# Expert layer: the shares of the experts spread over partitions by a transfer through DRAM instead of by TensorE products, with the router run further ahead

## The chip, the cores and the metric

The program runs on one core of one Trainium2 chip. Its engines are TensorE (PE, with its weight loads, PEld), VectorE (DVE), ScalarE (ACT), GpSimd (POOL) and SyncE (SP, which here only issues transfers). They run side by side, each takes its own instructions in order, and they wait for each other through semaphores. The metric is the device time of one execution in microseconds (us); "before" is the median of three runs.

## The reference, cut to what matters

The whole program is a network of twelve residual stages on a tensor `x` of 8 sequences x 512 tokens x 128 features. Only the stage with experts changes; it occurs twice, as the fourth and the sixth stage:

```python
    x = x + 0.5 * _L1_ffn_ref(_layernorm(x, axis=-1), ...)
...
        # 16 experts of 64 features, 4 chosen for a token, from 2 of 4 groups
        logits = xf @ gate_w.T
        scores = jax.nn.sigmoid(logits)
        sfc = scores + gate_bias
        ...
        topk_w = topk_w / (topk_w.sum(-1, keepdims=True) + 1e-20)
        topk_w = topk_w * SCALE
        cw = (jax.nn.one_hot(topk_idx, E, dtype=topk_w.dtype) * topk_w[..., None]).sum(1)
        hg = jnp.einsum('nh,eih->nei', xf, Wg)
        hu = jnp.einsum('nh,eih->nei', xf, Wu)
        act = jax.nn.silu(hg) * hu
        y = jnp.einsum('nei,ne,ehi->nh', act, cw, Wd)
        shared = jax.nn.silu(xf @ Ws_g.T) * (xf @ Ws_u.T) @ Ws_d.T
        y = y + shared
        return (x + y.reshape(b, s, h)).astype(hidden_states.dtype)
```

Here `cw` holds for each token the shares of the 16 experts: 0 for those that were not chosen, and otherwise the normalized score times 2.5. Every one of an expert's 64 features is multiplied by that token's share.

## The kernel before, in words

`x` stays in SBUF for the whole program, with tokens on the partitions (128 tokens x 4 chunks x 128 features for a sequence). The expert stage is `l1_ffn`. It works through the eight sequences in turn, and for each there are two generators, `routed` and `experts`, which `l1_ffn` steps in turn: one step of `experts(b)`, then one step of `routed(b + 1)`.

`experts(b)` computes with features on the partitions and the 512 tokens of the sequence along the free axis. All 16 experts are computed for every token. Two experts of 64 features fill the 128 partitions, so there are eight pairs, and as a ninth the shared expert. For each pair `e`, TensorE makes `pg` and `pu` (each a 128x512 product in float32, which runs as two passes, so the profile counts it as two instructions), ScalarE writes `act = silu(pg)`, VectorE multiplies `act` by `pu`, and then by the shares of the pair's two experts. TensorE multiplies the result by the down weights and sums over the nine into the PSUM bank `po`. At the end ScalarE copies `po` to `yT`, four transposes on TensorE turn it back to tokens, and VectorE adds it to `x` (`y`, then `add_half`).

The shares come out of the router with tokens on the partitions. `experts` needs the share of one expert along the tokens, and the same on all the 64 partitions of that expert's features. Before the change TensorE does that spreading: `shares` is a constant matrix of zeros and ones, and `pw = shares x shareT` (line 768, 32 rows against 128 columns, 512 tokens) repeats each row over 64 partitions. So that this keeps float32 precision[...], the share is cut in two terms, `share_lead` and `share_trail` (lines 723 to 726), which lie side by side in `halves` (copied four times by POOL, line 729, so that products can start from different row groups) and are transposed together (line 735). VectorE multiplies by `pw` in line 770.

`routed(b)` does what comes ahead of it: the layer norm of the sequence (`norm`: statistics and scaling on VectorE, the power -1/2 on POOL), four transposes and a copy on ScalarE to `xT` (tile `mm`, one PSUM bank that all transposes and router products share), and `route`: the products for the 16 scores, the sigmoid on ScalarE (a table of its own, so tables are loaded before and after it), then some 25 small VectorE instructions that rank groups and experts. The costly ones compare all pairs of 16 experts: two comparisons, a product on POOL (line 799), a maximum and a sum (lines 795 to 801). Last, the scores of the chosen are normalized to `share` (lines 847 to 853).

What order the instructions have on each engine is not that of the source: a scheduling layer takes the traced instructions, estimates their times and puts them in an order for each engine, and buffers are handed out from pools of a fixed number (`bufs`). A tile that wants a buffer in use waits for its last reader. Only in the second sequence (`b == 1`) are POOL and VectorE kept in the order of the source; there the steps of `aside`, which make constants for the attention stage that follows, are placed between. PSUM[...]: `mm` 1, `po` 1, `pg`, `pu` and `pw` 2 each. The buffers of `act` are 3.

SP issues the loads of weights. In the neighbourhood of the two stages it has one each: `w_ffn<-in_l2f` at the first's beginning, `w_mixer<-in_l3a` at the second's.

Of the kernel before, what the change touches and what calls it, by code (L numbers as in the profile page):

```python
# [25 lines left out]
P = 128  # L26
# [70 lines left out]
def _packs(i):  # L97
# [56 lines left out]
    p.add("spread", np.tile(np.repeat(np.eye(16, dtype=np.float32), 64, axis=1), (8, 1)))  # L154
# [68 lines left out]
class _Kernel:  # L223
# [459 lines left out]
    def l1_ffn(self):  # L683
# [3 lines left out]
        with ExitStack() as s:  # L687
            keep = s.enter_context(tc.tile_pool(name="keep", bufs=1))
            self.sb = s.enter_context(tc.tile_pool(name="sb", bufs=2))
            self.ps = s.enter_context(tc.tile_pool(name="ps", bufs=2, space=bass.MemoryType.PSUM))  # L690
            self.shares = keep.tile([P, 8, P], F32R, name="shares")
            nc.vector.tensor_copy(
                self.shares.rearrange("p e m -> p (e m)"), self.w["moe", "spread"]
            )
            self.seqs = [{} for _ in range(NB)]
            for _ in self.routed(0):
                pass
            for b in range(NB):
                ahead = self.routed(b + 1) if b + 1 < NB else iter(())
                experts = self.experts(b)  # L700
                for _ in range(10):
                    with self.in_order(*(() if b != 1 else (mybir.EngineType.Pool, mybir.EngineType.DVE))):
                        next(experts)
                        next(ahead, None)
                        if b == 1:
                            next(self.aside, None)
                for _ in ahead:
                    pass

    def routed(self, b):  # L710


        nc, sb, ps = self.nc, self.sb, self.ps
        q = self.seqs[b]
        q["xn"] = self.norm(self.x[b], self.ln_pool)
        yield
        xT = sb.tile([P, L], F32, name="xT")
# [5 lines left out]
        lead = sb.tile([P, NC, 16], F32R, name="share_lead")  # L723
        nc.vector.tensor_copy(lead, share)
        trail = sb.tile([P, NC, 16], F32, name="share_trail")
        nc.vector.tensor_tensor(trail, share, lead.bitcast(F32), ALU.subtract)
        halves = sb.tile([P, NC, 4, 2, 16], F32, name="halves")
        for k, t in enumerate((lead.bitcast(F32), trail)):
            nc.gpsimd.tensor_copy(
                halves[:, :, :, k, :], t.unsqueeze(2).to_broadcast([P, NC, 4, 16])  # L730
            )
        yield
        pt = ps.tile([P, NC, P], F32, name="mm", bufs=1)
        for c in range(NC):
            nc.tensor.transpose(
                pt[:, c, :], halves[:, c].rearrange("p r k e -> p (r k e)"), self.ident
            )
        q["shareT"] = sb.tile([P, L], F32R, name="shareT")
        nc.scalar.copy(q["shareT"], pt.rearrange("p c t -> p (c t)"))
        yield  # L740

    def experts(self, b):
# [11 lines left out]
        last = None  # L754
        for e in range(9):
            pg = ps.tile([P, L], F32, name="pg")
            self.mm(pg, w("w_g")[:, bass.ts(e, P)] if e < 8 else w("ws_g"), xT)
            pu = ps.tile([P, L], F32, name="pu")
            self.mm(pu, w("w_u")[:, bass.ts(e, P)] if e < 8 else w("ws_u"), xT)
            act = sb.tile([P, L], F32, name="act", bufs=3)  # L760
            nc.scalar.activation(act, pg, AF.Silu)  # L761
            nc.vector.tensor_tensor(act, act, pu, ALU.mult)  # L762
            if e < 8:
                if e % 2 == 0:
                    pw = []
                    for k in range(e, e + 2):
                        r = bass.ts(k % 4, 32)
                        pw.append(ps.tile([P, L], F32, name="pw"))
                        self.mm(pw[-1], self.shares[r, k, :], q["shareT"][r, :])
                nc.vector.tensor_tensor(act, act, pw[e % 2], ALU.mult)  # L770
            if last is not None:
                down(*last)
            last = (e, act)
            yield
        down(*last)
# [751 lines left out]
```

## Time and profile before

| | us |
|---|---|
| median of three runs | 2550.56 (2547.38 to 2552.48) |
| the profiled execution | 2548.84 |
| its span, from the first instruction to the last | 2547.1 |
| first expert stage, sequence 0 ends (copy of `yT`) | 596.56 |
| first expert stage, sequence 7 ends | 801.44 |
| second expert stage, sequence 0 ends | 1361.02 |
| second expert stage, sequence 7 ends | 1563.82 |
| busy in the whole span: PE, DVE, ACT, POOL | 2172.6, 1667.3, 1289.9, 645.0 |
| PE products `pw`, both stages | 128, of about 0.49 each |

A row of the profile such as "L770 DVE TENSOR_TENSOR act<-act,pw 128x512" is an instruction or a group: line of the kernel, engine, operation, what it writes and what it reads, and its size. In a timeline the first number is the start in us from the span's beginning and the second the length; "x2" says that two alike were put together; in brackets stands how long the engine was idle ahead of it, and what released it. In a table of windows each row gives the window's bounds and length and then, for PE, PEld, DVE, ACT and POOL, the busy time in it (with the number of instructions), the clock that TensorE was granted as a share of full speed, the share of time in which the transfer engines were busy, and GB/s. Lines of a matrix product or transpose are those of helpers (L256, L338), so products are told apart by the tiles that they write.

### The profile page before, as it was taken

Reading aid. Unit: us, or ns where it says so; the run is one execution under the profiler, and the core shown is the slowest. Engines: PE = TensorE matmul, PEld = TensorE weight load, DVE = VectorE, ACT = ScalarE, POOL = GpSimd, SP = SyncE. Lnnn points to the kernel's source line nnn. Section 1 sums busy time; section 2 is a strip of 40 time slices with the busy share of each in tenths; the row PEclk is TensorE's granted clock in tenths of the full one; section 3 lists DMA queues with packets and bytes.
Section 4 is the critical chain, followed back from the end, with each engine's and each line's share of the span. In section 5 each row is a group of like instructions: output and inputs, shape, how many; then the busy total and the mean of one; then the engine's idle time right before and its main releaser. Section 6 shows DMA issues by size and latency. Waiting matters only on the chain.

```text
span 2547.1 us, 30527 instructions
## 1 busy us (share of the span) xinstructions
PE 2172.6 (85%) x10959; PEld 1050.6 (41%) x10959; DVE 1667.3 (65%) x3908; ACT 1289.9 (51%) x2055; POOL 645.0 (25%) x916
## 2 busy tenths in 40 slices
PE   7579899879998988998879997763477999999989
PEld 3434444334444433333334443541354444444444
DVE  4565555468776888888638777975885466566611
ACT  3278787323332276777743333447343425555554
POOL 1122333112112011111122113545453112333330
PEclk9689798989999699999989998976788969999989
DMA  3000000000000000000000000000000000000001
GB/s 115 1 1 1 1 1 1 13 9 1 1 1 1 0 1 1 1 1 1 1 7 1 1 1 1 1 1 0 1 1 1 0 1 1 2 1 1 1 1 33
DMA packets 10039, 13.10 MB, mean 5 GB/s; under 512 B 416, under 2 KB 8736, under 8 KB 9760
## 3 DMA queue, kind: packets, MB, share of 16 engines
q1 hardware_dynamic: 7776, 10.11, 1.2%
q8 instruction: 86, 1.41, 0.2%
q10 hardware_dynamic: 2112, 1.05, 0.2%
q14 instruction: 65, 0.53, 0.1%
HBM read 9.06 MB, written 2.10 MB: 4 GB/s over the span
## 4 chain that ended last, share of the span: by engine, by line
PE 60%; DVE 18%; ACT 10%; POOL 7%; issue 4%; DMA 0%; ACTq 0%; DVEq 0%; POOLq 0%; SPq 0%
PE pair L256 11%; PE av L256 8%; PE po L256 8%; PE first L256 7%; PE pg L256 5%; PE pu L256 4%; PE ck L256 4%; PE mm L256 4%; DVE max L1282 3%; ACT e L1390 3%; PE ph L256 2%; POOL xn_rstd L271 1%; DVE xn L282 1%; PE pw L256 1%; PE pi L256 1%
## 5 line engine op out<-in xcount | busy, mean ns | idle before, releaser
L1282 DVE TENSOR_REDUCE max<-first 128x1 f32<-128x512 f32 (+3 forms) x864 | 534.9, 664 | 186.9 <-PE first L256 182.7
L1390 ACT ACTIVATE e<-pair 128x1024 f32<-128x1024 f32 (+3 forms) x512 | 436.4, 864 | 243.1 <-PE pair L256 230.8
L256 PE MATMUL first<-qkT 32*128 32x512 f32 (+3 forms) x1024 | 335.7, 471 | 32.8 <-DVE max L1282 32.1
L256 PE MATMUL pair<-qkT 32*128 32x512 f32 (+3 forms) x1024 | 223.3, 454 | 19.0 <-ACT e L1390 13.9
L256 PE MATMUL av<-e,v 128*32 128x512 f32 (+3 forms) x2048 | 237.8, 534 | 0.1
L761 ACT ACTIVATE act<-pg 128x512 f32<-128x512 f32 x144 | 86.0, 597 | 234.7 <-PE pg L256 186.0
L256 PE MATMUL pair<-mT,max_rows 32*128 32x512 f32 (+3 forms) x1024 | 191.0, 374 | 1.8 <-DVE mT L1324 1.8
L256 PEld LDWEIGHTS first<-qkT 32*128 32x128 f32 x1024 | 151.5, 196 | 97.8 <-DVE max L1282 89.7
L256 PEld LDWEIGHTS pair<-qkT 32*128 32x128 f32 x1024 | 95.4, 185 | 232.2 <-ACT e L1390 131.8
L1392 POOL TENSOR_SCALAR_AFFINE_SELECT e<-e 128x256 f32<-128x256 f32 x256 | 103.4, 407 | 251.7 <-ACT e L1390 251.4
L256 PE MATMUL po<-act,w_moe 128*128 128x512 f32 x288 | 157.3, 632 | 3.0 <-DVE act L770 1.9
L256 PE MATMUL pg<-xT,w_moe 128*128 128x512 f32 x288 | 153.5, 616 | 0.0
L256 PE MATMUL pu<-xT,w_moe 128*128 128x512 f32 x288 | 149.3, 601 | 0.0
L762 DVE TENSOR_TENSOR act<-act,pu 128x512 f32<-128x512 f32 x144 | 98.2, 682 | 49.0 <-PE pu L256 47.1
L1288 POOL COPY copies<-max 128x128 f32<-128x128 f32 x64 | 22.6, 410 | 341.0 <-DVE max L1282 341.0
L339 ACT COPY xT<-mm 128x512 f32<-128x512 f32 x80 | 46.4, 584 | 114.7 <-PE mm L338 102.4
L271 POOL TENSOR_TENSOR xn_rstd<-xn_rs,nhalf 128x4 f32<-128x4 f32 x80 | 88.9, 1111 | 54.4 <-ACT xn L277 35.2
L256 PEld LDWEIGHTS pair<-mT,max_rows 32*128 32x128 f32 x1024 | 96.8, 188 | 3.6 <-DVE mT L1324 3.3
L770 DVE TENSOR_TENSOR act<-act,pw 128x512 f32<-128x512 f32 x128 | 87.1, 682 | 16.5 <-PE pw L256 15.0
L282 DVE TENSOR_SCALAR xn<-x,xn_mv,xn_rstd 128x128 f32<-128x128 f32 x224 | 69.4, 370 | 39.4 <-POOL xn_rstd L271 27.9
L338 PE MATMUL mm<-w_const,xn 128*128 128x128 f32 x256 | 53.6, 331 | 48.0 <-DVE xn L282 43.6
L269 POOL TENSOR_SCALAR xn_rs<-xn_mv 128x4 f32<-128x4 f32 x80 | 20.4, 256 | 291.3 <-DVE xn_mv L267 289.7
(339 smaller groups left out, 4349.3 us busy)
## 6 DMA issues: line engine op xcount, KB each, us to landing
w_moe<-in_moe SPq DMA_DIRECT2D x1, 2392.0 KB, 14.0
out<-x SPq DMA_DIRECT2D x8, 256.0 KB, 2.3
x<-in_u ACTq DMA_DIRECT2D x4, 256.0 KB, 6.7
x<-in_u SPq DMA_DIRECT2D x4, 256.0 KB, 6.5
w_mixer<-in_l0a SPq DMA_DIRECT2D x1, 954.5 KB, 8.2
w_mixer<-in_l1a SPq DMA_DIRECT2D x1, 769.0 KB, 4.1
w_ffn<-in_l0f SPq DMA_DIRECT2D x1, 578.0 KB, 7.3
w_ffn<-in_l2f SPq DMA_DIRECT2D x1, 560.0 KB, 3.5
```

Source lines behind the costliest of these rows:

```text
L256: self.nc.tensor.matmul(out, lhsT, rhs, start=start, stop=stop)
L271: nc.gpsimd.tensor_tensor(rstd, rs, self.nhalf[:, :n], ALU.pow)
L282: nc.vector.tensor_scalar(xn[:, c, :], x[:, c, :], mv[:, c, 0:1], rstd[:, c : c + 1], ALU.subtract, ALU.mult)
L338: self.nc.tensor.transpose(pt[:, c, :], xn[:, c, :], self.ident)
L339: copy(out, pt.rearrange("p c t -> p (c t)"))
L761: nc.scalar.activation(act, pg, AF.Silu)
L762: nc.vector.tensor_tensor(act, act, pu, ALU.mult)
L770: nc.vector.tensor_tensor(act, act, pw[e % 2], ALU.mult)
L1282: nc.vector.tensor_reduce(mx[:, c, j, gs[0] : gs[-1] + 1], sc, AX.X, ALU.max, negate=True)
L1288: nc.gpsimd.tensor_copy(copies[:, :, :, :, g], mx[:, :, :, g].unsqueeze(3).to_broadcast([P, NC, 4, 8]),)
L1390: nc.scalar.activation(e[:, :, :n], sc[:, :, :n], AF.Exp, scale=scale)
L1392: nc.gpsimd.affine_select(e[:, :, :P], e[:, :, :P], pattern=[[0, 2], [1, P]], compare_op=ALU.is_ge, fill=0.0, base=0, channel_multiplier=-1,)
```

## The change: what it does

The share is no longer cut in two and spread by TensorE. It is transposed once per chunk to 16 rows (one for each expert), copied by ScalarE to `shareT` (16 partitions x 512 tokens), and written by SP to a DRAM tile of 32 KB, `shares`. SP then issues two transfers back from it into `share_wide`, a tile of 128 partitions x 8 pairs x 512 tokens (2 MB, 16 KB in a partition, two buffers): the first gives the rows of the even experts to each of partitions 0 to 63, the second those of the odd experts to partitions 64 to 127. VectorE multiplies `act` by a slice of `share_wide`. The constant `spread` (1024 columns of the weights) and its cast into `shares` are gone.

The routers form one chain of steps, of which 15 run ahead of the first `experts`: all of router 0 and, of router 1, everything up to the ranks. A router has nine steps and `experts` takes ten, so the lead grows by a step with each sequence. Because `pw` leaves two PSUM banks, `pg` and `pu` have three each; `act` has five buffers, and the down product follows its expert by three instead of one. The normalized sequence has its own tile `routed_xn` with three buffers, and `xT` has three too.

```diff
@@ -151,7 +151,6 @@
-    p.add("spread", np.tile(np.repeat(np.eye(16, dtype=np.float32), 64, axis=1), (8, 1)))
@@ -685,58 +684,57 @@
-            self.shares = keep.tile([P, 8, P], F32R, name="shares")
-            nc.vector.tensor_copy(
-                self.shares.rearrange("p e m -> p (e m)"), self.w["moe", "spread"]
+            self.dram = s.enter_context(
+                tc.tile_pool(name="dram", bufs=2, space=bass.MemoryType.DRAM)
             )
             self.seqs = [{} for _ in range(NB)]
-            for _ in self.routed(0):
-                pass
+            ahead = (step for b in range(NB) for step in self.routed(b))
+            for _ in range(15):
+                next(ahead)
             for b in range(NB):
-                ahead = self.routed(b + 1) if b + 1 < NB else iter(())
                 experts = self.experts(b)
                 for _ in range(10):
...
-                for _ in ahead:
-                    pass
...
-        q["xn"] = self.norm(self.x[b], self.ln_pool)
+        q["xn"] = self.norm(
+            self.x[b], self.ln_pool, out=sb.tile([P, NC, D], F32, name="routed_xn", bufs=3)
+        )
         yield
-        xT = sb.tile([P, L], F32, name="xT")
+        xT = sb.tile([P, L], F32, name="xT", bufs=3)
...
         share = out[0]
-        lead = sb.tile([P, NC, 16], F32R, name="share_lead")
-        nc.vector.tensor_copy(lead, share)
-        trail = sb.tile([P, NC, 16], F32, name="share_trail")
-        nc.vector.tensor_tensor(trail, share, lead.bitcast(F32), ALU.subtract)
-        halves = sb.tile([P, NC, 4, 2, 16], F32, name="halves")
-        for k, t in enumerate((lead.bitcast(F32), trail)):
-            nc.gpsimd.tensor_copy(
-                halves[:, :, :, k, :], t.unsqueeze(2).to_broadcast([P, NC, 4, 16])
-            )
-        yield
         pt = ps.tile([P, NC, P], F32, name="mm", bufs=1)
         for c in range(NC):
-            nc.tensor.transpose(
-                pt[:, c, :], halves[:, c].rearrange("p r k e -> p (r k e)"), self.ident
+            nc.tensor.transpose(pt[:16, c, :], share[:, c, :], self.ident)
+        shareT = sb.tile([16, L], F32, name="shareT")
+        nc.scalar.copy(shareT, pt[:16].rearrange("p c t -> p (c t)"))
+        rows = self.dram.tile([16, L], F32, name="shares")
+        nc.sync.dma_start(out=rows, in_=shareT)
+        q["share"] = sb.tile([P, 8, L], F32, name="share_wide")
+        pairs = rows.rearrange("(e k) t -> k e t", k=2)
+        for k in range(2):
+            nc.sync.dma_start(
+                out=q["share"][bass.ts(k, 64)],
+                in_=pairs[k].unsqueeze(0).to_broadcast([64, 8, L]),
             )
-        q["shareT"] = sb.tile([P, L], F32R, name="shareT")
-        nc.scalar.copy(q["shareT"], pt.rearrange("p c t -> p (c t)"))
+        yield
+        yield
         yield
@@ -751,28 +749,23 @@
-        last = None
+        acts = []
         for e in range(9):
-            pg = ps.tile([P, L], F32, name="pg")
+            pg = ps.tile([P, L], F32, name="pg", bufs=3)
...
-            act = sb.tile([P, L], F32, name="act", bufs=3)
+            act = sb.tile([P, L], F32, name="act", bufs=5)
             nc.scalar.activation(act, pg, AF.Silu)
             nc.vector.tensor_tensor(act, act, pu, ALU.mult)
             if e < 8:
-                if e % 2 == 0:
-                    pw = []
-                    for k in range(e, e + 2):
-                        r = bass.ts(k % 4, 32)
-                        pw.append(ps.tile([P, L], F32, name="pw"))
-                        self.mm(pw[-1], self.shares[r, k, :], q["shareT"][r, :])
-                nc.vector.tensor_tensor(act, act, pw[e % 2], ALU.mult)
-            if last is not None:
-                down(*last)
-            last = (e, act)
+                nc.vector.tensor_tensor(act, act, q["share"][:, e, :], ALU.mult)
+            acts.append((e, act))
+            if len(acts) > 3:
+                down(*acts.pop(0))
             yield
-        down(*last)
+        for last in acts:
+            down(*last)
```

## The prediction

> **What bounds the kernel now.** I read the summary of the page first, then a table of windows cut at the end of each sequence of the two expert stages (a sequence ends when ScalarE copies `yT`), then the timeline inside one sequence, then the timeline of the stage's start, and last the DMA issues. The first expert stage runs from about 545 to 803 us, the second from about 1309 to 1566 us; nothing else in the kernel is touched. The table, first stage, sequences 1 to 7 (columns: length, busy time of PE, weight loads, DVE, ACT, POOL, then granted clock):
>
> ```profile
> 596.56:629.53 32.97, 31.19 (x87) 13.46 (x86) 27.45 (x79) 10.52 (x17) 9.71 (x12) 1.00 0.00 0
> ...
> 715.29:744.91 29.62, 29.62 (x83) 12.78 (x82) 22.48 (x59) 9.81 (x15) 4.67 (x7) 1.00 0.00 1
> 744.91:774.54 29.63, 29.63 (x83) 12.78 (x82) 22.48 (x59) 9.81 (x16) 4.68 (x7) 1.00 0.00 1
> 774.54:801.44 26.90, 26.81 (x70) 11.01 (x68) 14.71 (x31) 6.44 (x11) 2.28 (x5) 1.00 0.00 1
> sum 204.88, PE 202.14 PEld 86.63 DVE 157.18 ACT 64.87 POOL 41.37; mean PE 28.88 PEld 12.38 DVE 22.45 ACT 9.27 POOL 5.91
> ```
>
> PE is busy for all of 29.62 us, at full clock; the second stage's seven windows sum to 202.8 us with PE busy 201.05. So TensorE work taken out comes off the time, until VectorE (22.48 of 29.62) fills up. What a share product costs, from the timeline of PE (start, length):
>
> ```profile
> 728.88 1.02 PE L256 MATMUL pu<-xT,w_moe 128*128 128x512 f32 x2
> 729.83 0.50 PE L256 MATMUL pw<-shareT,shares 32*128 32x512 f32 x1
> 730.26 1.12 PE L256 MATMUL pg<-xT,w_moe 128*128 128x512 f32 x2
> 731.32 0.50 PE L256 MATMUL pw<-shareT,shares 32*128 32x512 f32 x1
> 731.75 1.12 PE L256 MATMUL po<-act,w_moe 128*128 128x512 f32 x2
> 732.71 1.02 PE L256 MATMUL pu<-xT,w_moe 128*128 128x512 f32 x2
> ```
>
> A 128x512 product starts 0.857 us after the one before it where nothing lies between. From 728.88 to 732.71 are three of them and two `pw`: 3.83 - 3 x 0.857 = 1.26, or 0.63 us per `pw` slot. Two `pw` side by side (different row groups) fill one slot; the window from 715.29 has six slots.
>
> [...] No transfer here has 64 partitions; the trace's 128-partition loads reach 769 KB in 4.1 us. [...] one `xn` of normally 0.34 us took 1.80 beside a fill on POOL.
>
> ```profile
> 547.11 1.80 POOL L1092 MEMSET v<- 128x2048 f32 x1
> 547.19 1.80 DVE L282 TENSOR_SCALAR xn<-x,xn_mv,xn_rstd 128x128 f32<-128x128 f32 x1 [0.93 <-POOL xn_rstd L271]
> ```
>
> **Removed.** PE: all `pw`. Counting the instructions of the changed order between the `yT` transposes of sequences 0 and 7, first stage: 188 products of 0.857 = 161.1 us, and the small ones at their spacing in the window from 715.29 (6 share transposes of 0.43, 5 `xn` transposes of 0.44, 5 router products of 0.81, 7 `yT` of 0.58 = 12.9): 174.0 us, against 204.88 now. Second stage 174.1 against 202.8. So 30.9 and 28.7 us of cover are bought. DVE loses `share_lead` and `share_trail` (0.46 us a sequence) and the cast of `shares` (2.08 us, of which about 0.8 lay on the first stage's start). POOL loses `halves` (0.8 us, and 1.1 us of the router's chain). `act*pw` becomes `act*share` with both inputs in SBUF: 0.69 us for such a product (`fc`), 0.68 now; nothing.
>
> **Added: the DMA path, per sequence.** ScalarE copies 16 rows (0.58), SP stores 32 KB, waits for it, issues two reads of 1 MiB. Store: 2.3 us, the row of `out<-x`.
>
> ```profile
> out<-x SPq DMA_DIRECT2D x8, 256.0 KB, 2.3
> ...
> w_mixer<-in_l1a SPq DMA_DIRECT2D x1, 769.0 KB, 4.1
> ```
>
> Reads, from below: 1024 packets of 2 KB at the 85 ns that a 2068-byte packet of `w_heads` takes, over 16 engines: 5.4 us[...] Where the order puts the first `po` that needs it, 24 products (20.6 us) and 1.7 us of small ones lie between for sequences 2 to 4, more after: 22 us. Hidden, by 6 us. If it were not, `act*share` stands ahead of the next `act*pu` on DVE, `pu`'s three banks fill, and PE stops. SP carries nothing else there: the load of `l2f` was issued at 543.25, that of `l3a` at 1317.32, both ahead of the first share.
>
> **Added: the stage's start.** Now:
>
> ```profile
> 568.78 0.20 DVE L853 TENSOR_SCALAR share<-share 128x64 f32<-128x64 f32 x1
> ...
> 571.27 0.58 ACT L739 CAST shareT<-mm 128x512 fp32r<-128x512 f32 x1 [10.48 <-PE mm L735]
> ...
> 572.73 1.28 DVE L770 TENSOR_TENSOR act<-act,pw 128x512 f32<-128x512 f32 x2 [3.27 <-PE pw L256]
> 573.47 0.50 PEld L256 LDWEIGHTS po<-act,w_moe 128*128 128x128 f32 x2 [0.56 <-DVE act L770]
> 573.47 2.07 PE L256 MATMUL po<-act,w_moe 128*128 128x512 f32 x2 [0.15 <-DVE act L770]
> ```
>
> In the changed order PE does 16 products of sequence 0 first (10 now), and DVE does two `act*pu` and four `xn` more ahead of the share: ready at 568.98 - 0.8 + 1.2 + 1.0 = 570.4, copied by 572.4. But then, on DVE, router 1 complete and three instructions of router 2 stand ahead of the first `act*share`. With durations of router 0: `xn` transposes 1.1, copy 0.6, router product 1.9 (cold), sigmoid 0.25, router chain 12.7 (554.14 to 569.0 less its three `act*pu` and the waits they bring), share transposes 1.1, copy 0.6, then for router 2 again 1.1, 0.6, 1.9, 0.25, and 0.4 = 22.5 us: 594.9. The DMAs land at about 586, so they are not what is late; DVE's order is. First `po` at 595.7 against 573.47; from there 9 `po` and one `pg`, `pu` are left. 11 products are 9.4 us, and about 3 more because the clock is cold (now too, products go at half rate from 572 to 578): `yT` of sequence 0 at 608.2 against 596.56, 11.6 late. Second stage, without the cast's 0.8: 12.4 late, 1373.4 against 1361.02.
>
> **Added: VectorE close to full.** Summing the changed DVE order by the spacings of before (products 0.60, router's wide ones 1.15, waits for POOL's 2.36 us product where too little stands between) against PE, between updates of `x`: 39.2 to 36.1, 25.2 to 24.5, 28.3 to 25.4, 24.3 to 22.8, then PE is longer. Excess 8.2 us; second stage 4.4. The share's transposes stand in PE's queue, so PE waits when DVE is late. Blocking of `act*share` by POOL is estimated at 0.4 us a sequence and left out.
>
> **Sum.** First stage: 608.2 + 174.0 + 8.2 = 790.4 against 801.44, -11.0. Second: 1373.4 + 174.1 + 4.4 = 1551.9 against 1563.8, -11.9. Together -22.9 on the profiled execution's 2548.84 us (span 2547.1): 2525.9. The median of the runs, 2550.56, lies 1.7 higher: 2528.
>
> **Rivals.** (1) Slower: the reads[...]: four late in sequences 1 to 4 of each stage, and about 1 at the start, less where DVE's excess overlaps: some 14 us a stage, 28 in all, +5: 2556. It decides from about 19.5 us for the two reads (108 GB/s); at 50 GB/s the reads outlast a sequence and cost over 100 us. For it: nothing of this kind in the trace. Against: packets of 2 KB run at their 85 ns here. (2) No difference: DVE and PE wait for each other in turns, beyond the sums: 1.3 us a sequence more, 14 sequences, 18 us: 2546. For it: DVE at 92% by my sums, and its order puts few products into POOL's 2.36 us. Against: five `act` buffers and three of `pg`, `pu`. (3) Better: the start costs 4 us a stage and DVE hides: -(30.9 + 28.7) + 8 + 4 = -47: 2503. Against it, DVE's order at the start is fixed.
>
> **Chances and range.** Main case 0.68, (1) 0.15, (2) 0.10, (3) 0.07. Two runs 0.2% apart are what this kernel's measurement can tell from no change, 5.1 us. Faster: main but for 0.01, plus (3), plus a little of (2): 0.76. Same: 0.09. Slower: 0.15. Range 2510 to 2553: main, (2) and the near edge of (1). Main alone: 2514 to 2542.
>
> **What would show it.** No `pw`; windows of 22 to 28 us; first `act*share` near 595 and 1359 with PE idle some 15 us before it, released by DVE's router, not by a DMA; two reads landing within 12 us; PE waits on the share's transposes in the first four sequences. A first `act*share` of later sequences released by a DMA means rival 1. Shorter starts mean that I misread DVE's order.

## The result, and the profile after

The changed kernel takes 2539.25 us in the median of 20 runs (2531.5 to 2553.41), against 2548.75 us for the kernel before, run beside it; the ratio is 0.9969 with a 95% interval of 0.9954 to 0.9983. That is 7.9 us less (4.3 to 11.7; the ratio is that of the means, and the medians alone lie 9.5 us apart), where 22.9 were forecast: faster, but by a third of the forecast, and inside its range.

The profiled execution of the changed kernel took 2550.71 us (span 2549.0), longer than most of its runs, but a second profile of the same instructions (run 12 below, 2538.47 us) gave the four lengths in the table again to within 0.02 us, so the difference lies outside the stages. The two stages are therefore measured here from marks in their own neighbourhood: the last update of `x` ahead of the first stage; ahead of the second, VectorE's `o`, which takes up the last projection of the attention; and the copies of `yT`. "Start" is from the mark to the first `yT`, "steady" from the first to the eighth `yT`.

| us | start, stage 1 | steady, stage 1 | start, stage 2 | steady, stage 2 | sum |
|---|---|---|---|---|---|
| before | 50.99 | 204.88 | 52.26 | 202.80 | 510.93 |
| after | 60.64 | 188.80 | 63.86 | 191.45 | 504.75 |
| forecast for the change | +11.6 | -22.7 | +12.4 | -24.3 | -23 |
| measured for the change | +9.65 | -16.1 | +11.6 | -11.4 | -6.2 |

The starts came nearly as forecast. The steady stretches lost 46.9 us in the forecast and 27.4 on the chip: there the missing gain lies. The windows of the changed kernel's first stage, cut at `yT` as before:

```profile
611.05:638.72 27.67, 26.24 (x75) 12.00 (x74) 24.28 (x78) 9.91 (x15) 8.35 (x10) 1.00 0.40 78
638.72:666.89 28.17, 26.86 (x75) 11.82 (x74) 25.60 (x77) 9.92 (x15) 8.64 (x8) 1.00 0.38 76
...
723.24:752.03 28.79, 25.49 (x73) 11.43 (x72) 25.76 (x60) 9.32 (x15) 4.50 (x5) 1.00 0.38 75
752.03:776.15 24.12, 24.12 (x63) 10.83 (x62) 14.95 (x33) 6.54 (x12) 1.26 (x2) 1.00 0.45 88
776.15:799.85 23.70, 23.61 (x58) 10.19 (x56) 13.40 (x23) 5.96 (x10) 0.00 (x0) 1.00 0.00 1
sum 188.80, PE 179.92 PEld 80.31 DVE 150.38 ACT 62.08 POOL 35.80; mean PE 25.70 PEld 11.47 DVE 21.48 ACT 8.87 POOL 5.12
```

In the last two windows no router is left: TensorE is busy throughout, and a sequence takes 23.7 to 24.1 us. With a router in it a sequence takes 27 to 29, and neither TensorE nor VectorE is busy all of that time. What they wait for, in the steady stretch of stage 1 (the columns: total, times, longest):

```profile
POOL ge L792 <- DVE ge L790: 32.3, 9, 5.7
DVE act L760 <- PE pu L255: 12.8, 14, 1.2
DVE gt L793 <- POOL ge L792: 9.9, 7, 2.5
PEld po L255 <- DVE act L762: 7.0, 8, 1.9
PE mm L723 <- DVE share L846: 4.8, 5, 1.6
```

VectorE stands for GpSimd's product (9.9 us) and for TensorE's `pu` (12.8); TensorE stands for VectorE's `act*share` and, at the share's transposes, for its router. One such place from the timeline of stage 2, in the sequence that took 32.56 us:

```profile
1449.72 1.22 DVE L790 TENSOR_TENSOR ge<-masked 128x1024 f32<-128x1024 f32 x1
...
1451.02 2.73 POOL L792 TENSOR_TENSOR ge<-ge,w_moe 128x1024 f32<-128x1024 f32 x1 [2.84 <-DVE ge L790]
1451.46 0.68 DVE L760 TENSOR_TENSOR act<-act,pu 128x512 f32<-128x512 f32 x1
...
1453.79 1.23 DVE L793 TENSOR_TENSOR gt<-gt,ge 128x1024 f32<-128x1024 f32 x1 [1.65 <-POOL ge L792]
1454.93 0.68 DVE L762 TENSOR_TENSOR act<-act,share_wide 128x512 f32<-128x512 f32 x1
...
1455.67 1.15 PE L255 MATMUL po<-act,w_moe 128*128 128x512 f32 x2 [2.09 <-DVE act L762]
...
1456.63 1.89 PE L255 MATMUL pu<-xT,w_moe 128*128 128x512 f32 x2
...
1458.32 1.89 PE L255 MATMUL po<-act,w_moe 128*128 128x512 f32 x2
```

The `act*share` that TensorE needs had its inputs at 1452.2, but stands behind the maximum, which waits for GpSimd. TensorE stops for 2.09 us, and the products after it run at half rate for 3 to 4 us (1.69 us from one to the next at 1456.63, where 0.857 is usual; the table in the last section shows the clock there). The start, as the forecast described it (first stage):

```profile
575.22 0.20 DVE L846 TENSOR_SCALAR share<-share 128x64 f32<-128x64 f32 x1
...
576.71 0.57 ACT L725 COPY shareT<-mm 16x512 f32<-16x512 f32 x1 [7.51 <-PE mm L723]
...
592.12 0.20 DVE L846 TENSOR_SCALAR share<-share 128x64 f32<-128x64 f32 x1
...
598.62 3.09 DVE L762 TENSOR_TENSOR act<-act,share_wide 128x512 f32<-128x512 f32 x5
599.36 6.50 PE L255 MATMUL po<-act,w_moe 128*128 128x512 f32 x10 [1.55 <-DVE act L762]
```

Router 1 is done at 592.3 and three instructions of router 2 follow before the first `act*share`, at 48.2 us behind the mark (49.3 forecast). No wait for a transfer stands before it: SP issued the first of the two reads at 578.96 and the second at 579.68, and even at the longest time below, 12.5 us, both have landed by about 592. The time that the reads took, over both stages, from the query for the tile `share_wide`:

```profile
DMA to landing us min/median/max: 7.6/10.2/12.5
```

### The profile page after: what moved, and what is told of

It is laid out like the page before. It is cut to its first block, busy times and chain, and to the rows that moved or that the text cites. A ratio compares the mean times of both kernels' runs of the same rounds, so it can differ in the third digit from the quotient of the medians.

```text
span 2549.0 us, 30187 instructions
## 1 busy us (share of the span) xinstructions
PE 2135.1 (84%) x10786; PEld 1045.3 (41%) x10831; DVE 1659.8 (65%) x3874; ACT 1285.9 (50%) x2051; POOL 636.1 (25%) x884
## 4 chain that ended last, share of the span: by engine, by line
PE 54%; DVE 22%; ACT 10%; POOL 9%; issue 6%; DMA 0%; ACTq 0%; DVEq 0%; POOLq 0%; SPq 0%
PE pair L255 11%; PE av L255 8%; PE first L255 7%; PE po L255 6%; PE ck L255 4%; PE mm L255 3%; DVE max L1275 3%; ACT e L1383 3%; PE pg L255 3%; PE pu L255 3%; PE ph L255 2%; POOL xn_rstd L270 2%; DVE act L760 1%; POOL ge L792 1%; DVE xn L281 1%
## 5 line engine op out<-in xcount | busy, mean ns | idle before, releaser
L255 PE MATMUL po<-act,w_moe 128*128 128x512 f32 x288 | 147.7, 621 | 11.4 <-DVE act L762 10.1
L760 DVE TENSOR_TENSOR act<-act,pu 128x512 f32<-128x512 f32 x144 | 97.6, 680 | 29.2 <-PE pu L255 27.1
L1281 POOL COPY copies<-max 128x128 f32<-128x128 f32 x64 | 22.7, 410 | 344.8 <-DVE max L1275 344.8
L265 DVE BATCH_NORM_STATS2 xn_st<-x 128x6 f32<-128x128 f32 x320 | 80.5, 271 | 16.4 <-POOL x L1456 7.3
L762 DVE TENSOR_TENSOR act<-act,share_wide 128x512 f32<-128x512 f32 x128 | 89.8, 709 | 0.9
L255 PEld LDWEIGHTS po<-act,w_moe 128*128 128x128 f32 x288 | 54.5, 198 | 82.6 <-issue 45.8
## 6 DMA issues: line engine op xcount, KB each, us to landing
share_wide<-shares SPq DMA_DIRECT2D x32, 1024.0 KB, 10.2
w_moe<-in_moe SPq DMA_DIRECT2D x1, 1880.0 KB, 12.4
```

What stands on the lines that cost most here:

```text
L255: self.nc.tensor.matmul(out, lhsT, rhs, start=start, stop=stop)
L265: nc.vector.bn_stats(st[:, c, :], x[:, c, :])
L762: nc.vector.tensor_tensor(act, act, q["share"][:, e, :], ALU.mult)
```

## The experiments

Four theories were written down. **T** (turns): VectorE waits for GpSimd's product, TensorE for VectorE, VectorE for TensorE; that is what the steady stretch costs. **F** (full): VectorE simply has too much to do. **L** (lock): `act*share`, with two SBUF inputs, is shut out while GpSimd works (up to 2.35 us for one in the changed kernel, where the median is 0.68). **S** against **D**: the start is set by the order of the instructions, or by the transfers. In all runs marked "order held" the order of every engine's instructions within both stages was forced to that of the kernel it derives from, so that one thing alone changes; a list in the source does this, and shifts its line numbers. In this table "half clock" is how long TensorE's clock was granted at half within the two steady stretches, and the ratio is that of whole runs to the kernel before.

| run | start 1 | steady 1 | start 2 | steady 2 | half clock 1, 2 | ratio (95%) |
|---|---|---|---|---|---|---|
| after | 60.64 | 188.80 | 63.86 | 191.45 | 0, 3.4 | 0.9969 (0.9954-0.9983) |
| 1 no product | 56.69 | 179.07 | 60.12 | 179.63 | 0, 0 | 0.9833 (0.9813-0.9853) |
| 2 product on VectorE | 57.49 | 186.35 | 61.39 | 186.93 | 0, 0 | 0.9898 (0.9880-0.9915) |
| 3 no lock | 60.68 | 187.89 | 63.88 | 190.04 | 0, 3.4 | 0.9943 (0.9924-0.9962) |
| 4 sequence 0 by TensorE | 63.17 | 188.90 | 64.66 | 187.77 | 0, 0 | 0.9944 (0.9924-0.9964) |
| 5 start reordered | 55.89 | 190.07 | 58.72 | 193.61 | 0, 6.8 | 0.9912 (0.9897-0.9927) |
| 6 norm early | 60.65 | 186.51 | 59.45 | 189.51 | 0, 3.4 | 0.9954 (0.9939-0.9969) |
| 7 reads twice | 64.29 | 212.95 | 68.49 | 211.50 | 23.9, 23.9 | 1.0173 (1.0156-1.0190) |
| 8 before, no `pw` | 49.22 | 203.95 | 50.76 | 201.80 | 6.8, 6.8 | 0.9981 (0.9969-0.9992) |
| 9 before, lag 3 | 52.20 | 208.85 | 53.44 | 208.12 | 0, 0 | 1.0053 (1.0036-1.0069) |
| 10 before, no `pw`, lag 3 | 36.73 | 197.08 | 36.82 | 196.50 | 6.8, 3.4 | 0.9826 (0.9807-0.9846) |
| 11 runs 2, 5, 6 together | 53.72 | 183.65 | 54.46 | 185.35 | 0, 0 | 0.9870 (0.9850-0.9889) |
| 12 after, again | 60.64 | 188.82 | 63.84 | 191.44 | 0, 3.4 | 0.9961 (0.9946-0.9975) |
| 13 `act*share` first | 60.66 | 192.77 | 64.24 | 191.28 | 3.4, 3.4 | 1.0001 (0.9985-1.0017) |
| 14 the same, no lock | 60.66 | 191.83 | 63.58 | 188.03 | 6.8, 0 | 0.9986 (0.9974-0.9998) |
| 15 runs 5, 6, 14 together | 55.89 | 186.09 | 55.40 | 187.33 | 0, 0 | 0.9909 (0.9895-0.9924) |

The medians of whole runs follow the stages only to within some 10 us; part of that varies between executions of the same instructions, and these runs do not explain it. Causes are read from the stages. There too a difference of one or two us can be the clock's: a stretch of 3.4 us at half clock can cost up to 1.7 us (half of it, an estimate: products at half clock start 1.65 to 1.7 us apart in place of 0.857).

**1. The product left out** (order held). Equal scores then get wrong ranks.

```diff
-        nc.gpsimd.tensor_tensor(ge.rearrange(flat), ge.rearrange(flat), self.wide(before, m), ALU.mult)
```

> The changed kernel with GpSimd's product ge*before left out of the router (so equal scores are ranked wrongly; everything else is computed), and the order of every engine's instructions in both expert stages held to that of the changed kernel. Theory T (turns): in the steady stretch VectorE stands still for GpSimd's 2.36 us product (9.9 us in stage 1, 8.7 in stage 2), act*share is queued behind it, TensorE stops and restarts cold; without the product the two stretches from the first to the eighth yT come to about 180 and 180 us instead of 188.8 and 191.5: -15 to -20 us on the whole. Rival F (full): VectorE has simply too much to do; its busy time hardly falls, so less than 5 us is gained. Rival L (lock): the same gain as T, but then the PSUM kernel of this call gains too.

The steady stretches fell by 9.7 and 11.8 us to 179.07 and 179.63, as T said to within 1 us. Of the eight full-size products of a stage six lie in the steady stretch, so that one costs 1.6 us in stage 1 and 2.0 in stage 2 (where up to 1.7 of the 11.8 us can be the half clock that is gone). The starts fell by 4 us each, which had not been expected: there router 0's and router 1's products lie on the path. So the stages lost 29.2 us, and not the 15 to 20 that T had put on the whole. In this run's windows of stage 1, cut at `yT`, TensorE is busy almost throughout:

```profile
625.35:651.44 26.09, 26.09 (x75) 12.06 (x74) 25.21 (x77) 9.92 (x16) 5.70 (x6) 1.00 0.41 82
...
sum 179.07, PE 177.44 PEld 80.86 DVE 148.88 ACT 62.06 POOL 19.33; mean PE 25.35 PEld 11.55 DVE 21.27 ACT 8.87 POOL 2.76
```

The row is that of the same sequence as 638.72:666.89 of the changed kernel above: VectorE is as busy (25.21 us against 25.60), and yet the sequence is 2.1 us shorter. F is out as the main cause: with nearly the same work on VectorE the time fell. (L expects the same here; run 3 decides it.) The whole steady stretch is now TensorE's work: 177.44 of 179.07 us in stage 1, and 177.31 of 179.63 in stage 2.

**2. The product on VectorE** (order held; both sizes of it).

```diff
-        nc.gpsimd.tensor_tensor(ge.rearrange(flat), ge.rearrange(flat), self.wide(before, m), ALU.mult)
+        nc.vector.tensor_tensor(ge.rearrange(flat), ge.rearrange(flat), self.wide(before, m), ALU.mult)
```

> The changed kernel with that product done by VectorE in place of GpSimd, just ahead of the maximum that needs it, order otherwise held. VectorE gets 16 x (1.2 + 0.25) = 23 us more work and loses 18.6 us of waiting in the two steady stretches. T: the exchange is about even, -5 to +5 us. F: every microsecond added to a full VectorE counts, +12 us or more. L: all locking ends too: -5 us or better.

Faster than T expected: -2.4 and -4.5 us in the steady stretches, -3.2 and -2.5 in the starts, 12.6 in all, although VectorE gets 23 us of products more. So VectorE's busy time by itself doesn't set the time: what counts is how long the router's chain takes, 1.22 us for the product on VectorE against 2.36 and two hand-overs on GpSimd. Against run 1 both steady stretches are still 7.3 us longer. So the detour over GpSimd costs 2.4 and 4.5 us more than the product on VectorE does (up to 1.7 of the 4.5 can be the half clock), and the larger part of what run 1 gained is the product's being in the chain at all; how much of these 7.3 us is the longer chain, and how much VectorE's added work, these runs don't divide.

**3. No lock** (order held; sequences 1 to 7).

```diff
-            nc.vector.tensor_tensor(act, act, pu, ALU.mult)
+            part = pu if b and e < 8 else act
+            nc.vector.tensor_tensor(part, act, pu, ALU.mult)
             if e < 8:
-                nc.vector.tensor_tensor(act, act, q["share"][:, e, :], ALU.mult)
+                nc.vector.tensor_tensor(act, part, q["share"][:, e, :], ALU.mult)
```

> The changed kernel with act*pu written back into pu's PSUM bank for sequences 1 to 7, so that act*share reads PSUM and SBUF instead of two SBUF tiles and cannot be shut out by GpSimd; order held. L: the locked act*share (up to 2.35 us where 0.68 is normal) were what stopped TensorE: -6 us or better. T and F: the mean act*share is 0.71 against 0.68 us, 3 us over both stages, hardly on the path: within -3 to +2 us, the plus where pu's three banks are held longer.

The steady stretches gained 0.9 and 1.4 us. The lock is there (an `act*share` of 0.68 us took up to 2.35 in the changed kernel, and 0.69 at most in run 14, which has this edit too), but it is not the main cause.

**4. Sequence 0 spread by TensorE** (order free): for `b == 0` each share row is multiplied out by a float32 product `pg<-shareT` of 16 rows, three experts behind, into a bank of `pg`; no transfer.

> The changed kernel with the shares of sequence 0 of each stage spread by TensorE (eight products into pg's banks, weights of 16 partitions), sequences 1 to 7 by DMA as before; order free. If the start costs what the traces show (first yT 9.7 us later in stage 1 and 11.6 us later in stage 2 than before the change), most of it comes back, less what the eight products cost (at most 6.9 us a stage, part of it in TensorE's idle time): -8 to -18 us. If the start is bound by something else, by the norm's late start for example, -3 us or less.

The first weighted `act` came 19 and 17 us earlier, but the first `yT` 2.5 and 0.8 us later; the 8 to 18 us expected did not come. TensorE had stood still (for 2.02 us before 570.60), its clock was low (granted at half from 571.5 to 585.1), and the first of the added products ran at half rate (2.07 us each, 1.12 from 585.62 on), one at a time through `pg`'s banks. From the run's timeline, first stage:

```profile
572.91 2.07 PE L256 MATMUL pg<-shareT,w_moe 16*128 16x512 f32 x2
...
580.33 2.07 PE L256 MATMUL pg<-shareT,w_moe 16*128 16x512 f32 x2
...
582.44 0.69 DVE L764 TENSOR_TENSOR act<-act,pg 128x512 f32<-128x512 f32 x1 [4.10 <-PE pg L256]
```

**5. The start reordered.** VectorE: `share` of router 1, then seven `act*share` and two `act*pu`, then router 2. TensorE: share transposes, `po`, `xn` transposes, `po`, router product, `po` x3. Elsewhere held.

> The changed kernel with the order at the start of each expert stage written anew, all else held: on VectorE the first seven act*share of sequence 0 (and two act*pu) stand right behind router 1's share, ahead of router 2; on TensorE the po products of sequence 0 are put between router 2's small products instead of after them. Theory S (the start is set by the order of VectorE and TensorE, the transfers have landed): first act*share about 6 us earlier in each stage (592.4 in the place of 598.6), first yT 4 to 6 us earlier, -8 to -12 us on the whole. Rival D (the first transfers are what is late): first act*share moves by 1 us at most, within -2 to +2 us. Rival C (TensorE's cold clock eats it): first act*share 6 us earlier, yT less than 2 us earlier.

The first `act*share` came 6.4 and 6.1 us earlier and the first `yT` 4.75 and 5.1, as S said, without a wait for a transfer. D is out as the cause in the changed kernel; but the reads have only just landed here (the second, issued at 573.76, landed at 585.83), so little more is to be had this way. From the run's timeline:

```profile
586.20 0.20 DVE L917 TENSOR_SCALAR share<-share 128x64 f32<-128x64 f32 x1
586.31 3.09 DVE L833 TENSOR_TENSOR act<-act,share_wide 128x512 f32<-128x512 f32 x5
...
587.35 1.91 PE L311 MATMUL po<-act,w_moe 128*128 128x512 f32 x2
```

The steady stretches gave 1.3 and 2.2 us of it back, so that the stages together gained 6.5 us, less than the 8 to 12 expected.

**6. The norm early** (order held).

```diff
-        q["xn"] = self.norm(
-            self.x[b], self.ln_pool, out=sb.tile([P, NC, D], F32, name="routed_xn", bufs=3)
-        )
+        q["xn"] = self.norm(self.x[b], self.ln_pool)
```

> The changed kernel with the routed normalisation kept in the kernel-wide pool, as before the change, instead of in the stage's own; order within the stages held. Theory N: in stage 2 the new tile could be written only when the attention's memory was free, so VectorE's twelve routed_xn came after the last yn, beside three GpSimd products that shut them out (5.96 us), and the first pg came 12.9 us after the attention's last projection in the place of 8.35: about 4.5 us come back in stage 2, none in stage 1, -3 to -5 us on the whole. Rival: the norm's place is covered by the clock and by router 0, within -1 to +1 us.

The start of stage 2 became 4.4 us shorter, that of stage 1 stayed. In the changed kernel the tile belonged to the stage's own memory, and VectorE wrote it last, beside three GpSimd products (changed kernel, timeline of stage 2):

```profile
1313.52 5.96 DVE L281 TENSOR_SCALAR routed_xn<-x,xn_mv,xn_rstd 128x128 f32<-128x128 f32 x12
...
1320.44 2.05 PE L255 MATMUL pg<-xT,w_moe 128*128 128x512 f32 x2
```

Here the first `pg` starts 8.36 us behind the mark (1315.55 - 1307.19), as before the change (8.35), against 12.9 in the changed kernel. That the steady stretches gained 2 us each was not expected. The median of whole runs did not show the gain: in this run's profile the part between the stages, from the first's last `yT` to the second's mark, was longer, 514.3 us against 507.7 in the changed kernel and again in run 12. It was longer in the other two runs with this edit too (511.8 in run 11, 513.5 in run 15), but also in runs 9 and 10 without it (515.8 in both). Why is not known.

**7. Both reads issued twice** (order held): `for k in (0, 1, 0, 1)` in place of `range(2)`.

> The changed kernel with both reads of 1 MiB issued twice for each sequence, one pair behind the other, order held. The second pair lands about 8 to 10 us later than the reads of the changed kernel. By the predicted cover of 6 us (and 6.5 to 8 us between landing and first use in the trace of sequences 2 and 3), act*share of sequences 2 to 4 then waits 2 to 4 us for a transfer, and the start moves by up to 2 us a stage: +5 to +15 us. If the transfers had no slack at all: +8 us for each of 16 sequences, +100 us or more. If they had far more slack than worked out: 0.

The expectation of 5 to 15 us was far too low: +52 us in the stages. The second read of each half, which writes the same place, is held back until the first of that half has landed (the four issues of a sequence span 13.4 to 13.7 us, the two of the changed kernel 1.25 to 1.35), and the second pair lands 10.2 us behind the first, as expected. The run's waits from 605 to 860 us, total, times and longest:

```profile
DVE act L834 <- DMA share_wide<-shares: 20.3, 6, 4.9
PE po L312 <- DVE act L834: 17.4, 6, 4.6
```

With 10.2 us more, `act*share` waits 3.4 us on average (20.3 / 6), so some 7 us had been free, near the 6 of the forecast. In the changed kernel's own trace the second read of sequences 2 to 4 of stage 1 lands 7.6, 6.0 and 8.0 us ahead of its first use. What the expectation had wrong is how often the wait is paid, and what follows it: it was put on three sequences, and six waits were paid in the steady stretch of stage 1 alone; and TensorE, which stands meanwhile, has its clock granted at half for 23.9 us of each steady stretch, which can be up to 12 of the 24 us and 10 of the 20 us that these stretches grew by (an estimate: half of the time at half clock that was added).

**8. Before, without `pw`** (order held; the router does not weight the output).

```diff
-                        pw.append(ps.tile([P, L], F32, name="pw"))
-                        self.mm(pw[-1], self.shares[r, k, :], q["shareT"][r, :])
+                        pw.append(xT)
```

> The kernel before the change with only the pw products left out: act is multiplied by xT in the place of the spread share (so the output is not weighted by the router), order of everything else held. It measures the first step of the sum by itself: 28 to 31 us of TensorE work a stage. If TensorE's sum alone sets the time afterwards, first to eighth yT comes to 174 us in each stage (204.9 and 202.8 before): -59 us. Theory T: with the same VectorE order and the same waits for GpSimd, VectorE takes over well before: 183 to 190 us a stage, -25 to -40 us on the whole.

This is the most telling run. 64 products a stage gone, and the steady stretches are 0.9 and 1.0 us shorter. T had said 183 to 190 us, TensorE's sum 174. TensorE was busy for 29.62 of 29.62 us before, but in part with `pw` while it would otherwise have waited for VectorE: in the steady stretch of stage 1 its `po` waited for VectorE's second product for 0.7 us before, and for 14.9 us here. The window of this run that answers to that one:

```profile
738.56:768.74 30.18, 27.78 (x75) 12.46 (x74) 22.19 (x59) 9.82 (x15) 5.12 (x8) 0.94 0.00 0
```

And from its timeline of TensorE, where it now stands for VectorE, and its clock falls:

```profile
731.98 1.12 PE L314 MATMUL po<-act,w_moe 128*128 128x512 f32 x2 [2.07 <-DVE act L842]
732.94 1.85 PE L314 MATMUL pg<-xT,w_moe 128*128 128x512 f32 x2
734.59 1.91 PE L314 MATMUL pu<-xT,w_moe 128*128 128x512 f32 x2
```

Two side effects take something off this run: `act*xT` reads two SBUF tiles, and is shut out beside GpSimd (up to 2.34 us for one, where 0.68 is usual; 4.2 us more than `act*pw` over both stages, and GpSimd's products take 2.64 us on average in place of 2.36), and the half clock can cost up to 3.4 us a stage. Together these are some 8 us a stage at most (an estimate), and not the 28 or more that are missing.

**9. Before, with the lag of three alone** (order free): `acts`, five buffers, `if len(acts) > 3`, as in the change.

> The kernel before the change with one part of the change alone: down-projections three experts behind in place of one, five act tiles in place of three; pw, its banks and the router stay as before. Theory I (the two parts need each other): TensorE has pw to do while VectorE finishes an act, so a longer lag finds nothing to fill: first to eighth yT 200 to 206 us in each stage (204.9 and 202.8 before), -3 to +3 us on the whole. Rival: the lag by itself is worth something, -8 us or better.

Slower, by 4.0 and 5.3 us in the steady stretches, outside the 200 to 206 expected; why stays open.

**10. Before, without `pw` and with the lag of three** (order free; the router does not weight the output; `pg` and `pu` three banks).

> The kernel before the change without pw (act is multiplied by xT, so the output is not weighted by the router) and with the lag of three, five act tiles and three banks each for pg and pu; no transfers, router as before. With the lag of one the same removal gave 1 us a stage. Theory I: with the lag TensorE no longer stands behind VectorE at every expert, and first to eighth yT comes to 183 to 191 us a stage as in the changed kernel, -25 to -38 us on the whole, since the start costs nothing here. Rival (VectorE is the bound whatever the lag): 200 us or more a stage, within 5 us of the kernel without pw and with the lag of one.

197.1 and 196.5 us: 7 and 5 us below the same with a lag of one, but short of the 183 to 191 expected. (The short start is no result: nothing there waits for a share.) The lag by itself cost time (run 9), and without `pw` it pays, together with the third banks and the free order. The last 8 and 5 us to the changed kernel's 188.8 and 191.45 are not assigned: its router differs (further ahead, no `halves`), but in run 10 sequence 0 ends before router 1 is done, so that seven of the router's products lie in each steady stretch and not six. The stretches are thus not alike, and no run divides this. In run 10 TensorE still stands for the transposes of `halves`, once for 2.98 us.

**11. Runs 2, 5 and 6 together.**

> The changed kernel with the three edits that paid put together: the product ge*before on VectorE, the order at the start written anew, the norm in the kernel-wide pool. Sum of their parts in the traces: -12.6 (product), -9.9 (start), -4.4 (norm in stage 2): -27 us against the changed kernel if they add, 2512; -18 us (2521) if the shorter router and the new start overlap.

2517.49 us, 0.987 of the kernel before; in the stages the three add up (27.6 us less than the changed kernel; 27 expected). This version beats both kernels.

**12. The changed kernel again,** with its order written out.

> The changed kernel, instruction for instruction, with its order written out as a list: how far its stages and its time repeat. Expected: first to eighth yT within 2.5 us of 188.8 and 191.5, first act*share 48.2 us behind the last update of x, median within 3 us of 2539.

The stages and the median (2538.71 us) came as expected.

**13 and 14. `act*share` ahead of the waiting maximum,** in ten of sixteen routers, with two SBUF inputs and then with PSUM.

> The changed kernel with VectorE's order alone altered in ten of the sixteen routers: the act*pu and act*share that stood behind the maximum (which waits for GpSimd's product) are put ahead of it, into the 2.36 us of that product. Theory Q (the wait costs because act*share is queued behind it): TensorE gets its act some 2 us earlier in each such sequence, first to eighth yT 183 to 186 us instead of 188.8 and 191.4, -8 to -14 us on the whole. Theory QL (queue and lock together): the act*share put there has two SBUF inputs and is shut out until GpSimd is done, so it ends hardly earlier than behind the maximum: -3 to +3 us.

> The same order, with act*pu kept in pu's PSUM bank for sequences 1 to 7, so that act*share can run beside GpSimd's product. The lock alone gave 0.9 and 1.4 us in the two steady stretches. QL: only both together pay: 182 to 186 us a stage, -8 to -14 us against the changed kernel. Q: the same as with the order alone, to within 2 us a stage. If neither queue nor lock is what makes the product cost 10 to 12 us a stage: 187 us or more in both.

The 8 to 14 us did not come: 192.8 and 191.3, then 191.8 and 188.0. Run 14 lost 3.0 us in stage 1 and won 3.4 in stage 2, of which the half clock (6.8 us in place of none, none in place of 3.4) can be up to 3.4 and 1.7; 187 us or more in both is what was expected if neither the queue nor the lock makes the product cost. VectorE now hardly waits for GpSimd, but TensorE stops no less: in run 13 it is idle for 11.8 us of stage 1's steady stretch, against 8.9 in the changed kernel. Run 13's waits in that stretch:

```profile
DVE act L831 <- PE pu L311: 18.2, 16, 2.2
...
PE mm L794 <- DVE share L917: 6.1, 5, 2.0
...
PEld po L311 <- DVE act L833: 4.5, 6, 1.9
...
DVE gt L864 <- POOL ge L863: 1.6, 3, 0.7
```

Against the changed kernel the wait for GpSimd fell from 9.9 to 1.6 us and that for `act*share` from 7.0 to 4.5, while the waits for the router's `share` rose from 4.8 to 6.1 and VectorE's for `pu` from 12.8 to 18.2. Both uses of VectorE stand in TensorE's one queue; whichever VectorE does second makes TensorE stop. The queue position in the example above is where the wait shows, not what it costs. That the two take turns is read from these waits and not tested by itself; what runs 1 and 2 show is that the product's place in the router's chain costs time.

**15. Runs 5, 6 and 14 together.**

> The order of the two runs above with PSUM for act*pu, the start written anew and the norm in the kernel-wide pool; GpSimd keeps its product. If the parts add: start -9.9, norm in stage 2 -4.4, steady stretch -8 to -14: 2511 to 2517 us, as fast as the three edits with the product on VectorE (2517). If the queue theory fails: 2522 to 2526.

2526.02 us, where 2522 to 2526 were expected if the queue is not the cause: better than the changed kernel mostly through its starts (13.2 of the 20.0 us that the stages gained), but 7.5 us behind run 11 in the stages; run 11 has the shorter router.

## Why the prediction was wrong

**TensorE's work as the bound** ("So TensorE work taken out comes off the time, until VectorE (22.48 of 29.62) fills up"): the size of a `pw` slot stands, the inference is too simple. Run 8 took the same work out by itself, with the lag of one, and got 1 us a stage instead of 31 and 29, although VectorE was busy for only 22.19 of 30.18 us there: its chain to the next `act` was at once behind. With the lag of three, and with GpSimd's product gone too (run 1), the steady stretches are 25.8 and 23.2 us shorter than before the change. A window with TensorE busy throughout says that removing work *may* pay; it doesn't say how far behind the next bound is.

**TensorE's sum in the new order,** 174.0 and 174.1 us: in run 1, where TensorE stands for only 1.6 and 2.3 us, it is 177.44 and 177.31, so 3.4 and 3.2 too low.

**"VectorE close to full", +8.2 and +4.4 us: the step that failed.** What stands above TensorE's own 177.4 and 177.3 us in the changed kernel is 11.4 us in stage 1 and 14.1 in stage 2. Most of it goes when GpSimd's product leaves the router's chain, 9.7 and 11.8 us, although VectorE keeps its work (run 1); 2.4 and 4.5 us go when VectorE takes the product over (run 2). I had summed VectorE's busy time and its waits over a whole sequence and compared the sum with TensorE's; that lets a surplus of one engine in one place pay for a lack in another, across a queue that is too short for it (this is read from the waits; no run tests it by itself). In stage 2, where the sum was smallest, it was most wrong. That is rival 2, "DVE and PE wait for each other in turns", which had a chance of 0.10: 1.3 us a sequence were put on it, and measured were 1.4 (188.8 - 182.2 and 191.45 - 178.5, 19.6 us over 14 sequences). But 6.6 of the 19.6 us are TensorE's sum, so that 0.9 us a sequence are left for the turns, and it is in part luck that the two numbers meet. Against rival 2 I had set five `act` buffers and three banks; the share's transposes stand in TensorE's queue and no buffer lets them pass. Rival 3, VectorE hidden and a cheap start, was wrong in both.

The account closes: 6.65 us from TensorE's sum and 12.9 from this step, less 2.75 by which the starts cost less than forecast, are the 16.8 us between the forecast of -23 and the -6.2 measured in the stages.

**The start,** +11.6 and +12.4 us: measured +9.65 and +11.6, with the mechanism as told (run 5: VectorE's order and TensorE's, not the transfers). In stage 2 some 4.4 us of it had a cause that I had not seen, the late norm (run 6), and the part that I had seen was as much smaller, 7.2 us; that the total came within 0.8 us there is luck.

**The transfers:** hidden, as told. What the forecast put on the reads, and with it the landing at 586 and the cover of 6 us, was my estimate; the trace of before shows no such transfer. The cover came out at some 7 us by run 7, and at 6 to 8 in the trace. The first of a pair lands 7.7 us after its issue and the second 12.2 (medians), and between the two landings are 5.1 us, 1 MiB at 206 GB/s. The 5.4 us that the prediction worked out from below were too few, and so what was set against rival 1 was wrong: a packet of 2 KB took 171 ns in these reads (median), not the 85 of `w_heads`. Rival 1's slower reads did not come, and its price was too low: in run 7 `act*share` waited 3.4 us on average, near the four that rival 1 put on a sequence, and the run lost 52 us and not 28, since the wait comes again from sequence to sequence.

**The lock,** estimated at 0.4 us a sequence and left out: 0.9 and 1.4 us a stage (run 3). The trace shows it in `act*share`, which reads two SBUF tiles, beside GpSimd's product (2.35 us, where the median is 0.68). The `xn` shown in the prediction (1.80 us) has only one full tile among its inputs. Leaving the lock out did little harm.

**Signs of failure that I named** were transfers and a shorter start, and no bound on TensorE's waits per sequence. One sign did speak: windows of 22 to 28 us were named, and five of the fourteen are longer, up to 32.56.

## What to carry to other kernels

A fully busy engine is the bound only as far as the next engine's chain is away; test that by leaving the work out before counting its whole time as gain. When two engines feed each other through in-order queues, add up the longest chain between them (here scores to share, with each hand-over), not busy times per period. A detour to a third engine in such a chain costs time though that engine is mostly idle: GpSimd's product of 2.36 us cost 1.6 to 2.0 us a router here, and moving it back paid even though it made a nearly full engine fuller.

## What the runs showed of the hardware

In these runs a pause of about 2 us was in places enough to halve TensorE's clock, and its length alone didn't decide. After the 2.09 us at 1455.67, and after the 2.07 at 731.98 in run 8, the products started 1.65 to 1.7 us apart, instead of 0.857, for 3 to 4 us. After 1.73 us (1484.19 in the changed kernel) they did not, nor after one of 2.40 in run 8. In the stages of all these runs every stretch at half clock is a multiple of 3.41 us long. With windows of that length laid on the clock's steps, for PE alone, the changed kernel shows (length, busy time, clock):

```profile
1449.81:1453.23 3.42, 3.33 (x8) 1.00 0.03 6
1453.23:1456.64 3.41, 1.32 (x4) 1.00 0.00 0
1456.64:1460.05 3.41, 3.41 (x6) 0.50 0.00 0
```

The pause lies within one window, in which TensorE is left busy for 39%, and the window after it runs at half. The longer pause of run 8, from 643.15 to 645.55, is shared by two windows, and the clock stays:

```profile
640.83:644.24 3.41, 2.32 (x6) 1.00 0.00 0
644.24:647.66 3.42, 2.11 (x5) 1.00 0.00 0
```

In the steady stretches of the changed kernel and of run 8 half clock followed all five windows that were busy for 39%, and none of the others, which were busy for 49% or more. So in these two runs the place of a pause on the 3.41 us grid counted beside its length. Where the bound lies is not shown: in runs 7, 10 and 13 windows between 41 and 50% went either way.

The four lengths of the stages repeat to 0.02 us between two profiles of the same instructions, while the part ahead of the first stage differed by 6 us and the part behind the second by 6.
